# Four-layer graph network, layer 0: padding the rows of four DRAM tables and one SBUF tile, and making a table's second copy on the chip

## The chip, the core and the metric

The kernel runs on one core of one Trainium2 chip. A core has five engines: PE (matrix multiply), DVE and ACT (vector and scalar work), POOL (general elementwise work) and SP, which here only issues transfers. Sixteen DMA engines carry out all transfers, whichever engine issued them. The metric is device time in microseconds (us), from launch to end, and lower is better.

## What is computed

There are 64 graphs (B) of 256 nodes (N) with 256 features (D). Four layers follow one another, and after each comes `x = layernorm(x + layer(x))`. Layer 0 is the one that is changed. It is a recurrence over the nodes; `norm_adjT` is the adjacency transposed and scaled by `dinv`:

```
def step(h, i):
    x = jnp.take(h_e, i, axis=1)
    row = jnp.take(norm_adjT, i, axis=1)
    x_par = jnp.einsum('bj,bjd->bd', row, h)
    iou = x @ W_ioux.T + b_ioux + x_par @ W_iouh.T + b_iouh
    r, z = jnp.split(iou, 2, axis=1)
    r, z = (jax.nn.sigmoid(r), jax.nn.sigmoid(z))
    hc = jnp.tanh(x @ W_coux.T + b_coux + x_par * r @ W_couh.T + b_couh)
    h_new = z * x_par + (1.0 - z) * hc
    h = jax.lax.dynamic_update_slice(h, h_new[:, None, :], (0, i, 0))
```

Step i needs the states that the steps before it have made, so the 256 steps run one after another. Layers 1 to 3 (a graph convolution and two attentions) work on one graph at a time, and have no such order.

## The kernel before

**Setup.** The sums that each node receives from nodes that don't depend on the recurrence are matrix products (`x_product`). They are written to the DRAM table `Us` (`x_out`), for the first half of the nodes before the loop and for the second half inside it (`x_side`).

**The loop.** `for now in range(N)` runs the 256 steps under a schedule written out by hand: what stands first in the text is issued first on its engine. Eight steps (U) make a block, 32 steps (T) a table. Within a step, p is the place in the block and i the place in the table. A step goes from PE to ACT to PE to DVE and back: transpose the parent sum, multiply (`h_part`), sigmoid, transpose, multiply, tanh, combine. On POOL, `ready` (the parent sum of the next step) stands in the same order as POOL's other work.

**Parent sums.** A block's sums stand in a tile `ACC`, loaded from `Us` two blocks ahead (`sums_in`, line L316). Newly made states add to it in three ways:
- near nodes at once, by DVE (`push`, L628) and POOL (`push_far`, L661 and L665);
- states of the last 64 nodes or so by small products on PE (`late`, L519), from the ring of states `Hw` and the masked adjacency table `An`. The result `lb` goes to the DRAM table `Lb` (L499) and comes back as `late_sb` in another layout (L505); POOL adds it in the two last steps of the block before (L874);
- older states by `early_fill` (L418). Their rows `Hs` come from the DRAM table of states `Hd` (`early_load`, issued through `next_load`, L269), the results go to `Es` (L430) and come back as `early_sb` (L447).

**Tables.** For the next table, `late_load` brings the adjacency columns into `raw`, 64 rows in a ring. `raw` is needed twice, in partitions 0 to 63 and 64 to 127, one for each half of the features, so each piece was loaded twice from DRAM, in runs of 32 values. In the steps i = 20 to 22 POOL multiplies `raw` by a mask into `An` (`cut`, L477). `load_S` loads another table once and doubles it by a transfer within SBUF (`S<-S`, L547).

**Transfers.** Nearly all are issued by SP in the order of the text; one that waits holds back those behind it. Transfers for later are put into a list (`load_later`) from which `next_load` takes two in each of the first four steps of a block. New states go into the ring `Hw` by two small transfers a step (`into_ring`, L654), and a quarter of the way from a table's end 32 rows of the ring are written out to `Hd` (`flush`, L636). `load_x` brings the x rows of a block into `xq` (L567).

The DRAM tables `Us`, `Es`, `Lb` and `Hd` are dense. A load that takes eight consecutive rows of 128 values from one of the first three finds 4096 contiguous bytes, and a load of eight rows of 256 values from `Hd` finds 8192; `xq` takes four rows of 1024 bytes into 4096 contiguous bytes of a partition.

**Layers 1 to 3** read `Hd` once more, a graph at a time (`y<-Hd`, L1043).

Of the kernel before, what the change touches and what calls it, by code (L numbers as in the profile page):

```python
# [9 lines left out]
F32 = mybir.dt.float32  # L10
# [9 lines left out]
P = 128  # L20
# [50 lines left out]
def _recurrence(tc, ident, Hd, x, adj, W_ioux, b_ioux, W_iouh, b_iouh, W_coux, b_coux, W_couh, b_couh, wide, then):  # L71
# [19 lines left out]
    nc = tc.nc  # L91
# [12 lines left out]
    with ExitStack() as ctx:  # L104
# [100 lines left out]
        )  # L205

        dram = ctx.enter_context(tc.tile_pool(name="r_dram", bufs=2, space=bass.MemoryType.DRAM))
        Us = dram.tile([2, B, N, P], F32, name="Us", bufs=1)

        def x_product(pb, at, A, Xs):  # L210

# [38 lines left out]
        def next_load(n):  # L250
            if loads:
                loads.pop(0)[1](n)
# [125 lines left out]
        def early_load(e, got=[]):  # L378

            _, k, lo, hi, t = early.pop(e)  # L380
            rows = hi - lo
            if t == 0:
                Es[k, lo] = dram.tile([2, NG, 4, T, P], F32, name=f"Es_{k}_{lo}", bufs=1)
            Hs = wide.tile([P, GB, D], F32, tag="wide", name=f"Hs_{k}_{lo}_{t}")
            last = [load_later(
                Hs[0:rows], Hd[lo:hi, t * GB:(t + 1) * GB, :], 1
            )]
            if t % 2 == 0:
                A = stream.tile([P, 2 * GB, T], F32, tag="A", name=f"A_{k}_{lo}_{t}")
                last.append(load_later(  # L390
                    A[0:rows],
                    adj[t * GB:(t + 2) * GB, lo:hi, k * T:(k + 1) * T].rearrange("b j i -> j b i"), 1
                ))
                got[:] = [A]
            early_in.append((last, k, lo, hi, t, Hs, *got))
# [58 lines left out]
        def late_load(k, n=None):  # L454
# [6 lines left out]
                nc.gpsimd.memset(raw, 0.0)  # L461
            begun = []
            for lo, hi, at in ring(max(first, 0), last):
                for o in range(2):
                    to = raw[o * W + at:o * W + at + hi - lo]
                    of = adj[:, lo:hi, k * T:(k + 1) * T].rearrange("b j i -> j b i")
                    if n is None:
                        nc.scalar.dma_start(to, of)
                    else:
                        begun.append(load_later(to, of, 1.5))  # L470

            def cut(lo):
                while not all(begun):
                    next_load(now)
                part = raw[:, lo:lo + B // 4].rearrange("p b (s u) -> p b s u", u=U)
                take = window[k % 2].rearrange("p (s u) -> p s u", u=U).unsqueeze(1)
                nc.gpsimd.tensor_mul(  # L477
                    An[:, lo:lo + B // 4].rearrange("p b u s -> p b s u"), part,
                    take.to_broadcast(list(part.shape)),
                )  # L480

            for e in range(4):
                if n is None:
                    cut(e * B // 4)
                else:
                    at_step(n + (20, 21, 21, 22)[e], lambda e=e: cut(e * B // 4))
            return An

        def late(first):
# [1 line left out]
            k, i = divmod(first, T)  # L491
            An = tables[k]["An"]
            lb = stream.tile([P, NG, D], F32, tag="lb", name=f"lb_{first}", bufs=1)
            Lb = dram.tile([2, NG, 4, U, P], F32, tag="Lb", name=f"Lb_{first}")
            sides[first] = blk.tile([P, U, P], F32, tag="late", name=f"late_sb_{first}", bufs=1)

            def send():
# [63 lines left out]

        def load_x(a):

            xq = stream.tile([P, U // 2, D], F32, tag="xq", name=f"xq_{a}")
            for h in range(2):
                at = a * U + h * U // 2
                nc.sync.dma_start(xq[h * B:(h + 1) * B], x[:, at:at + U // 2, :])  # L567
            return xq

        def flip_x(a, e, xq):  # L570
# [850 lines left out]
def kernel(ctx: ExitStack, tc: tile.TileContext, ins, out):  # L1421
# [4 lines left out]
    dram = ctx.enter_context(tc.tile_pool(name="dram", bufs=1, space=bass.MemoryType.DRAM))  # L1426
    ident = main.tile([P, P], F32, name="ident")
    make_identity(nc, ident)
    Hd = dram.tile([N, B, D], F32, name="Hd")
    l2, l3 = (  # L1430
        {w + n: ins[f"{l}_gnn_{w}{n}"] for w in "Wb" for n in "vkqo"} for l in ("L2", "L3")
    )
# [55 lines left out]
```

## Time and profile before

| | |
|---|---|
| median of 3 runs | 3435.97 us (3435.91 to 3440.31) |
| the profiled execution | 3432.33 us, its span 3430.6 us |
| granted PE clock in it, mean | 0.968 |
| setup, 0 to 142 us | 142 us, DMA engines 0.97 busy |
| recurrence, 142 to 1560 us | 1418 us, PE 1257.3 us busy, DMA engines 0.66 busy |
| layers 1 to 3, from 1560 us | 1870.6 us, PE 1832.3 us busy, DMA engines 0.20 busy |

The span runs from the first instruction to the last of one execution; the device time has 1.7 us around it. A wait is idle time of an engine ahead of an instruction, with what ended it; `issue` stands for a wait that no event in the profile explains. Queue q1 is that of SP and carries most of the data; q8 and q14 carry instructions. In the transfer view, "under 512 B" and the like count packets cumulatively, and the share is that of the sixteen engines' time in the window.

### The profile page before, as it was taken

How to read it: one execution, taken by the hardware profiler on the slowest of the kernel's cores; microseconds unless marked ns; L12 is line 12 of the kernel's file. 1: busy time of each engine (PE TensorE's matmuls, PEld its weight loads, DVE VectorE, ACT ScalarE, POOL GpSimd, SP SyncE). 2: the span in 40 equal slices, each digit the busy share in tenths (PEclk: the TensorE clock that was granted, in tenths of full speed). 3: DMA queues.
4: the chain of work that ended last, by engine and by line, in shares of the span. 5: the costliest groups of instructions: out<-in, count | busy, mean ns of one | idle time of the engine just before them, and what ended most of it. 6: DMA issues, size and time to landing. Idle time of an engine off the chain costs nothing.

```text
span 3430.6 us, 86707 instructions
## 1 busy us (share of the span) xinstructions
PE 3171.4 (92%) x32424; PEld 2391.6 (70%) x32424; DVE 2571.3 (75%) x7381; ACT 1836.5 (54%) x4754; POOL 1862.5 (54%) x2165
## 2 busy tenths in 40 slices
PE   5699989888888898886999999999999999999997
PEld 4566656555555666665888888888888888888885
DVE  3477767776675777774888888888888888888885
ACT  0154545444444454443666666666666666666664
POOL 2376767766575778762444444444444444444443
PEclk8899999999998999998999999999999999999999
DMA  9856676777987575422122222222222222222210
GB/s 299 227 160 146 167 175 162 166 177 181 205 195 175 143 179 139 128 73 75 47 56 56 56 56 57 58 59 59 58 56 58 56 58 59 56 57 59 57 32 20
DMA packets 595503, 368.82 MB, mean 108 GB/s; under 512 B 282236, under 2 KB 561928, under 8 KB 590344
## 3 DMA queue, kind: packets, MB, share of 16 engines
q1 hardware_dynamic: 576360, 346.19, 40.1%
q10 hardware_dynamic: 18720, 17.04, 1.5%
q8 instruction: 259, 4.24, 0.5%
q14 instruction: 164, 1.34, 0.1%
HBM read 244.45 MB, written 99.61 MB: 100 GB/s over the span
## 4 chain that ended last, share of the span: by engine, by line
PE 79%; DVE 6%; DMA 6%; issue 4%; SPq 2%; POOL 2%; ACT 1%; DVEq 0%; ACTq 0%; POOLq 0%
PE mm L995 13%; PE rc L603 7%; PE rc L595 5%; PE late L519 4%; PE s L1193 4%; PE mm_2f L995 4%; PE mm_3v L995 3%; PE mm_3f L995 3%; PE mm_2v L995 3%; PE mm_t L995 3%; PE mm_2s L995 3%; PE mm_g L995 3%; PE mm_2w L995 3%; PE o L1228 3%; PE z_ps L603 3%
## 5 line engine op out<-in xcount | busy, mean ns | idle before, releaser
L1205 POOL TENSOR_TENSOR p3s<-p 128x256 f32<-128x256 f32 x512 | 358.3, 731 | 365.1 <-ACT p L1203 365.1
L628 DVE SCALAR_TENSOR_TENSOR ACC<-keep,S,ACC 128x128 f32<-128x128 f32 x1712 | 478.8, 342 | 17.3 <-POOL ACC L874 11.7
L995 PE MATMUL mm<-xT,weights 128*128 128x256 f32 x2048 | 484.3, 385 | 2.7 <-ACT xT L1092 2.7
L995 PEld LDWEIGHTS mm<-xT,weights 128*128 128x128 f32 x2048 | 386.7, 191 | 79.9 <-issue 25.5
L1202 DVE TENSOR_TENSOR p<-s,neg 128x512 f32<-128x512 f32 x512 | 317.5, 682 | 118.8 <-PE s L1193 118.8
L665 POOL TENSOR_TENSOR ACC<-ACC,far 128x384 f32<-128x384 f32 (+1 forms) x313 | 371.8, 1188 | 24.5
L803 POOL TENSOR_TENSOR ready<-ACC,dinv 128x128 f32<-128x128 f32 x255 | 101.8, 399 | 378.2 <-DVE ACC L628 370.1
L661 POOL TENSOR_TENSOR far<-hs,S 128x384 f32<-128x384 f32 (+1 forms) x313 | 304.3, 972 | 4.7
L1203 ACT ACTIVATE p<-p 128x512 f32<-128x512 f32 x512 | 292.3, 626 | 1.6 <-DVE p L1202 1.6
L959 ACT ACTIVATE y<-y,shift,rstd 128x256 f32<-128x256 f32 x512 | 272.9, 599 | 26.2 <-DVE shift L957 22.5
L595 PE MATMUL rc<-WxT,xqT 128*64 128x256 f32 x2048 | 283.2, 399 | 1.1 <-issue 1.0
L1117 ACT ACTIVATE qk<-mm,weights 128x256 f32<-128x256 f32 x256 | 107.3, 470 | 301.7 <-PE mm L995 301.7
L1106 POOL TENSOR_TENSOR y<-y,g 128x512 f32<-128x512 f32 x64 | 81.0, 1266 | 301.2 <-issue 301.2
L603 PE MATMUL rc<-WhT,rT 128*64 128x128 f32 x2048 | 176.8, 295 | 54.0 <-DVE rT L826 47.2
L1242 DVE RECIPROCAL rT<-o 128x256 f32<-128x256 f32 x128 | 223.7, 1748 | 0.3 <-PE o L1219 0.2
L822 ACT ACTIVATE rs<-rc 128x128 f32<-128x128 f32 x256 | 70.9, 277 | 283.0 <-PE rc L603 283.0
L519 PE MATMUL late<-Hw,An 64*32 64x128 f32 x7680 | 182.0, 282 | 41.8 <-issue 39.8
L947 DVE BATCH_NORM_STATS2 st<-y 128x6 f32<-128x256 f32 x512 | 209.4, 409 | 13.1 <-POOL y L1106 10.2
L826 DVE TENSOR_TENSOR rT<-rT_ps,xpT 128x128 f32<-128x128 f32 x256 | 74.0, 289 | 181.5 <-PE rT_ps L824 179.8
L951 POOL TENSOR_TENSOR rstd<-rstd,mhalf 128x2 f32<-128x2 f32 x256 | 173.6, 695 | 48.9 <-DVE rstd L950 33.9
L603 PEld LDWEIGHTS rc<-WhT,rT 128*64 128x64 f32 x2048 | 111.7, 141 | 125.0 <-DVE rT L826 93.0
L603 PE MATMUL rc<-WhT,xpT 128*64 128x128 f32 x2048 | 174.6, 291 | 25.8 <-ACT xpT L612 19.1
(162 smaller groups left out, 7347.0 us busy)
## 6 DMA issues: line engine op xcount, KB each, us to landing
xX<-in_x_dram ACTq DMA_DIRECT2D x16, 1024.0 KB, 7.4
Us<-xu SPq DMA_DIRECT2D x64, 256.0 KB, 4.2
xq<-in_x_dram SPq DMA_DIRECT2D x64, 256.0 KB, 6.7
ACC<-Us SPq DMA_DIRECT2D x32, 512.0 KB, 6.5
Es<-eu SPq DMA_DIRECT2D x64, 256.0 KB, 3.3
early_sb<-Es SPq DMA_DIRECT2D x32, 512.0 KB, 5.6
xin<-in_x_dram SPq DMA_DIRECT2D x64, 256.0 KB, 2.9
ad<-in_adj_dram SPq DMA_DIRECT2D x64, 256.0 KB, 3.3
```

Of the source, the lines that this page charges most:

```text
L519: nc.tensor.matmul(pb[o][q * T:(q + 1) * T, e, :], An[rows, b].rearrange("p u s -> p (u s)"), Hw[rows, b, :], start=True, stop=True,)
L595: nc.tensor.matmul(G[o * B:(o + 1) * B], xqT[a, i // 2][:, i % 2, kc, h * B:(h + 1) * B], WxT[:, kc, o, gates], start=False, stop=False, s ...
L603: nc.tensor.matmul(G[o * B:(o + 1) * B], hT[:, kc * B:(kc + 1) * B], WhT[:, kc, o, g], start=False, stop=(kc == 1), skip_group_check=True,)
L628: nc.vector.scalar_tensor_tensor(acc[:, 0, :], keep[:, j % 2, :], s, acc[:, 0, :], ALU.mult, ALU.add)
L661: nc.gpsimd.tensor_mul(tmp[:, 0:count, :], hs.unsqueeze(1).to_broadcast(shape), s.unsqueeze(2).to_broadcast(shape),)
L665: nc.gpsimd.tensor_add(acc, acc, tmp[:, 0:count, :])
L959: nc.scalar.activation(y[:, c, :], y[:, c, :], AF.Identity, bias=shift[:, c:c + 1], scale=rstd[:, c:c + 1],)
L995: nc.tensor.matmul(pm[:, c, :], lhsT[:, k, c * P:(c + 1) * P], rhs[:, k, :], start=(k == 0), stop=(k == 1),)
L1202: nc.vector.tensor_add(p, s_ps[i], self.neg3)
L1203: nc.scalar.activation(p, p, AF.Exp, scale=ISQ)
L1205: nc.gpsimd.tensor_add(both, p[:, 0, :], p[:, 1, :])
L1242: nc.vector.reciprocal(rT, o_ps[:, 1, :])
```

## The change

The four DRAM tables get 64 unused values behind each row, so that a row no longer touches the next, and only the used part is addressed. The tile `xq` gets 4 unused values behind each row. A transfer of several rows, which went in runs of 4096 or 8192 bytes, goes in runs of 512 bytes (`Us`, `Es`, `Lb`) or 1024 bytes (`Hd`, `xq`); the bytes are the same. The adjacency columns are loaded into `raw` once, and a transfer within SBUF copies partitions 0 to 63 to partitions 64 to 127, at step i = 17 of the table before, or for the first table at once.

```diff
-        Us = dram.tile([2, B, N, P], F32, name="Us", bufs=1)
+        Us = dram.tile([2, B, N, P + 64], F32, name="Us", bufs=1)[..., 0:P]
...
-                Es[k, lo] = dram.tile([2, NG, 4, T, P], F32, name=f"Es_{k}_{lo}", bufs=1)
+                Es[k, lo] = dram.tile(
+                [2, NG, 4, T, P + 64], F32, name=f"Es_{k}_{lo}", bufs=1
+            )[..., 0:P]
...
             for lo, hi, at in ring(max(first, 0), last):
-                for o in range(2):
-                    to = raw[o * W + at:o * W + at + hi - lo]
-                    of = adj[:, lo:hi, k * T:(k + 1) * T].rearrange("b j i -> j b i")
-                    if n is None:
-                        nc.scalar.dma_start(to, of)
-                    else:
-                        begun.append(load_later(to, of, 1.5))
-
-            def cut(lo):
+                to = raw[at:at + hi - lo]
+                of = adj[:, lo:hi, k * T:(k + 1) * T].rearrange("b j i -> j b i")
+                if n is None:
+                    nc.scalar.dma_start(to, of)
+                else:
+                    begun.append(load_later(to, of, 1.5))
+
+            def double():
                 while not all(begun):
                     next_load(now)
+                nc.sync.dma_start(raw[W:], raw[0:W])
+
+            def cut(lo):
...
+            if n is None:
+                double()
+            else:
+                at_step(n + 17, double)
...
-            Lb = dram.tile([2, NG, 4, U, P], F32, tag="Lb", name=f"Lb_{first}")
+            Lb = dram.tile([2, NG, 4, U, P + 64], F32, tag="Lb", name=f"Lb_{first}")[..., 0:P]
...
-            xq = stream.tile([P, U // 2, D], F32, tag="xq", name=f"xq_{a}")
+            xq = stream.tile([P, U // 2, D + 4], F32, tag="xq", name=f"xq_{a}")
...
-                nc.sync.dma_start(xq[h * B:(h + 1) * B], x[:, at:at + U // 2, :])
+                nc.sync.dma_start(xq[h * B:(h + 1) * B, :, 0:D], x[:, at:at + U // 2, :])
...
-    Hd = dram.tile([N, B, D], F32, name="Hd")
+    Hd = dram.tile([N, B, D + 64], F32, name="Hd")[:, :, 0:D]
```

## The prediction

> **What bounds the kernel now.** I read the stage table first, then PE's waits in the long middle stage, then the transfers in windows with and without those waits, then SP's rows.
>
> ```profile
> q8 instruction: 259, 4.24, 0.5%
> ...
> 0.00:142.00 142.00, 81.71 (x319) 64.30 (x320) 39.66 (x62) 4.54 (x7) 29.39 (x23) 0.81 0.97 291
> 142.00:1560.00 1418.00, 1257.34 (x19819) 852.13 (x19817) 1034.72 (x3608) 658.07 (x2186) 981.20 (x1055) 0.96 0.66 159
> 1560.00:3430.60 1870.60, 1832.30 (x12290) 1475.18 (x12290) 1496.87 (x3711) 1173.86 (x2561) 851.88 (x1088) 0.99 0.20 55
> ```
>
> Columns: window, PE, weight loads, DVE, ACT, POOL (busy, instructions), granted clock, DMA share, GB/s. Layers 1 to 3 are PE at work (1832 of 1871 us) with idle DMA engines: nothing is to be had there. The recurrence has 161 us in which PE is idle. Queue q8 carries 4.24 MB in 259 packets. PE has 32,424 matmuls and as many weight loads, 65 bytes each on that account: q8 is PE's instruction fetch, 250 instructions a packet.
>
> ```profile
> PE late L519 <- issue: 39.8, 22, 6.4
> PE rc L603 <- issue: 10.8, 7, 3.0
> PE z_ps L603 <- issue: 9.3, 4, 3.7
> PE z_ps L595 <- issue: 8.1, 3, 4.8
> PE rc L595 <- issue: 1.0, 1, 1.0
> ...
> 508.31 0.65 PE L519 MATMUL late<-Hw,An 64*32 64x128 f32 x8 [6.36 <-issue]
> ```
>
> These 37 waits (69.0 us) have no releaser. The last line shows one: it falls inside 32 equal products on tiles long at hand, so no operand can be missing. What can be missing is the instruction. Two windows in which the DMA engines are full tell when:
>
> ```profile
> DMA packets 1049, 1.56 MB, mean 156 GB/s; under 512 B 831, under 2 KB 831, under 8 KB 911
> q1 hardware_dynamic: 1047, 1.54, 104.0%
> q8 instruction: 1, 0.02, 1.1%
> ...
> DMA packets 3214, 2.16 MB, mean 308 GB/s; under 512 B 44, under 2 KB 3069, under 8 KB 3213
> q1 hardware_dynamic: 3213, 2.14, 100.4%
> q8 instruction: 1, 0.02, 0.9%
> ```
>
> The first is 496 to 506 us, before the 6.36 us wait: 80 packets of 2 to 8 KB and 138 of 8 KB or more (one is the fetch) carry nearly all the bytes. The second is 813 to 820 us, a flush of `Hd` in runs of 512 bytes: just as full, twice the rate, and PE has no wait at all. Over more places:
>
> ```profile
> sum 90.00, PE 57.07 PEld 38.07 DVE 51.05 ACT 28.00 POOL 42.01; mean PE 6.34 PEld 4.23 DVE 5.67 ACT 3.11 POOL 4.67
> ...
> sum 49.00, PE 48.57 PEld 34.15 DVE 33.12 ACT 25.19 POOL 33.88; mean PE 6.94 PEld 4.88 DVE 4.73 ACT 3.60 POOL 4.84
> ```
>
> The first sums nine 10 us windows with long runs in flight (from 314 us to 1248 us; DMA share 0.88 to 1.08, 126 to 236 GB/s): PE idle 33 of 90 us. The second sums the seven flush windows (share 0.78 to 1.02, 202 to 314 GB/s): idle 0.4 of 49 us. The bound that can move is therefore PE's fetch behind full queues, worst behind long runs.
>
> **The change part by part.**
>
> *Long runs split.* Engine time per byte: the flush window spends 1.004 x 16 x 7 = 112 us on 2140 kB, 53 ns per kB; the first window 166 us on 1540 kB, 108 ns per kB; 909 to 917 us (161 packets of 8 KB or more and 139 of 4 KB, 102.3%, 1.88 MB) 70. The fetch itself took 1.1% of 160 us, 1.8 us, in the first and 0.9% of 112, 1.0 us, in the flush. Split are all 64 loads of `Hs` (36.9 MB), 94 of `ACC`, `early_sb`, `late_sb` (49 MB) and 64 of `xq`; the runs of `rows` (4096), `S` and `raw` (128) and the copies within SBUF stay. What can be won: 69.0 us of waits, and the slow clock after them (508.3 to 513.3 us has 0.67), for which I put 0.7 us on each of the 22 or so over 1.2 us: 15. Ceiling 84. By bytes, some 90% of the first window is split, less elsewhere, and raw, S and rows still fill the queue: I take 60%, -50 us. Bounds: 0 (delay set by bytes queued, whatever the run) and -84, or -104 with some 20 us of waits on `Lb`, `Hs` and `Hw` transfers standing in those queues.
>
> Two rules of the Trainium skill speak against this. "Runtime: NRT & Kernel Launch", Instruction fetch mechanics, says that refills of 256 instructions are prefetched and their cost mostly hidden: by it the term is 0 and the whole change +8. The refill size agrees (250); the hiding does not (69 us), and the row decides. "DMA: Bandwidth & Descriptors", Why small descriptors are slow, charges each packet about 3 cycles over its bytes/32: 19 for 512 bytes, 131 for 4096, so 16% more per byte; on 49 MB at about 310 GB/s (159 us of all engines) that is an estimated +22 us of DMA time. A lone 128-partition load of 4096-byte runs reaches 350 to 440 GB/s in its best slices (206 to 212 us), against 300 to 350 for the flush: that agrees, 0.3 us a load, +29 us for 94. But the mixed windows above, where it matters, pay 70 to 108 ns per kB: 36.9 MB of `Hs` at 17 ns less (70 to 53) is 627/16 = -39 us. Net about 0, and with 34% of DMA time idle none of it is on the path, except `late_sb`: 30 loads 0.3 us later, of which the waits show three ending a POOL wait: +1.
>
> *Raw loaded once.*
>
> ```profile
> L269 SPq DMA_DIRECT2D raw<-in_adj_dram x26: 343/2564/11215, 148.7 to 1279.9; - x26
> L636 SPq DMA_DIRECT2D Hd<-Hw x24: 609/1196/7390, 266.8 to 1534.0; - x24
> L316 SPq DMA_DIRECT2D ACC<-Us x32: 377/414/1879, 130.0 to 1440.3; - x32
> S<-S SPq DMA_DIRECT2D x7, 328.0 KB, 8.9
> ```
>
> SP is held 2.6 us (median) by each of 26 loads; 13 go, 8 copies come: SP issues 5 transfers fewer, ACT one fewer. Some 28,700 packets of 128 bytes go, 512 of 8192 bytes come. SP's hold was not on the path: 0 for it; what the queue gains is in the 60%. The copy (512 KB) has no row; the nearest is `S<-S`, 3.9 us in quiet (256 KB), 8.9 in traffic (328 KB). By bytes 8 to 14 us. It is issued at i = 17 and POOL wants it at i = 20, three steps of 4.9 us: cover 14.7. Ready copies cost 0; if one lands late, POOL waits at `cut`, behind it stands `ready`, and DVE and PE wait for that. Six tables by 0 to 3 us: 0 to +18, I take +3. Behind the copy on SP stand `rows`, `A`, `Hs`, `xq` of that step, wanted a block later: 0.
>
> *First table.* Here the wait is on the path:
>
> ```profile
> 129.89 11.80 DMA raw<-in_adj_dram
> ...
> 141.82 4.99 POOL An L477 x4
> ...
> 146.87 1.80 POOL raw L461
> 148.67 0.37 POOL ready L803
> ```
>
> One load instead of two should land between 135.5 (half) and 141.7; then SP's copy of 512 KB, 5 to 9 us: ready 1 us earlier to 9 later; I take +4. SP waits meanwhile with the side loads `xA`, `xX`, `rows` behind it, first used at 159 us: 0.
>
> *No cost:* the stores to the padded tables go in the same 512-byte runs; PE reads the same rows of `xq`; `y<-Hd` keeps 1024-byte runs, with PE's 1832 us as cover (2.8 us to landing, a graph ahead; exposed, 64 x some tenths).
>
> Sum against the profiled execution: 3432.3 - 50 + 1 + 3 + 4 = 3390. The median of the runs stands 3.6 us above that execution: 3394.
>
> **The rivals.**
> 1. *The fetch is delayed by the bytes ahead of it, not by the run.* For it: a fetch also waits when 128-byte runs fill the queue, and a packet of several short runs may hold an engine as long as one long run did. Against: the flush windows. Then only the halved `raw` helps, at most 28,700 x 16 ns/16 = 29 us of DMA time, perhaps 8 us of waits, against +8: 3436.
> 2. *Slower: packets hold SP.* The transfers of many packets (`raw` up to 3072, `Hd` up to 2048) hold SP up to 11.2 and 7.4 us; `ACC` with 128 only 0.4. After the change `ACC`, `early_sb` and `late_sb` have 1024 and `Hs` up to 896. A block issues five or six of them just ahead of `Lb` and `Hw`. If each holds SP 1 to 2 us more, `Lb` goes some 6 us later and `late_sb` misses POOL's addition. The slack there is about 7 us in a good block (issued 1165.3, 5.0 to landing, added 1177.0) and none in the worst. At 3 us over, in 30 blocks, +90: 3394 + 90 - 40 (queue thinner) = 3444. It decides once holds exceed the slack by 1.5 us on average. Against: SP's holds are mostly the same bytes draining, and these drain faster.
> 3. *Raw copies land late in every table*: 15 us after issue plus 8 would cancel the gain; `raw` itself took 14.3 at most. 3436 to 3445.
> 4. *Nearly all fetch waits go*, and the transfer waits with them: 3345.
>
> **How the numbers follow.** Forecast (and the part of 4 on its side) 0.75; rival 1 0.10, of which half within the band; rival 2 0.11; rival 3 0.04. About 0.2%, 7 us, is what can be told from no change. Faster by more: 0.75 and a little of rival 1, 0.77; the same 0.06; slower 0.17. The range reaches from rival 4 a little beyond (the -104 bound gives 3340) to the first third of the slower cases: 3335 to 3444.
>
> **What would show it.** PE's waits on issue in the recurrence fall from 69 to under 30 us; q1 has about 677,000 packets instead of 576,360 (84,000 more for 94 loads, 32,000 for `Hs`, 12,000 for `xq`, 28,000 fewer for `raw`) at nearly the same bytes; bursts at i = 1 to 3 and 9 to 11 move over 250 GB/s; layers 1 to 3 keep 1871 us. I am wrong in the size if the waits on issue stay above 50 us (rival 1), in the sign if POOL's waits on `late_sb` (11.8 us now) grow past 60 (rival 2) or its waits on `raw` past 50 (rival 3).

## The result: no change, where 42 us less were forecast

The changed kernel took 3438.93 us (median of its runs, 3417.72 to 3454.21) beside 3435.92 us of the kernel before on the same chip. The ratio is 1.001, with a 95% interval of 0.9988 to 1.0032: no change that can be told. The forecast was 3394. The profiled execution below is the slowest of the changed kernel's runs (3454.21 us), so up to 15 us of it are its own; times are compared by medians further down.

The changed kernel's first queue and its stages (columns as before: window, then PE, weight loads, DVE, ACT, POOL, granted clock, DMA share, GB/s):

```profile
q1 hardware_dynamic: 677912, 346.85, 41.4%
```

```profile
142.00:1580.00 1438.00, 1258.70 (x19805) 853.89 (x19804) 1031.84 (x3608) 658.30 (x2185) 980.95 (x1055) 0.95 0.69 157
1580.00:3452.40 1872.40, 1834.89 (x12290) 1475.65 (x12290) 1495.55 (x3711) 1175.07 (x2561) 851.79 (x1088) 0.99 0.20 55
```

The change does what it says: 677,912 packets, where the prediction had about 677,000. Layers 1 to 3 keep their length (1872 us; 1871 before). So everything happens in the recurrence, where PE's waits in 142 to 1580 us are now these (engine, tile and line, what it waited for, us in total, times, longest). `rc` on `rT` is the step's own product that waits for the transposed factor which DVE hands it:

```profile
PE rc L611 <- DVE rT L834: 65.7, 62, 7.8
PE late L527 <- issue: 37.6, 18, 5.4
...
PE xpT_ps L618 <- DVE xp L872: 11.4, 24, 5.0
PE z_ps L611 <- issue: 7.9, 3, 3.6
PE early L420 <- DMA Hs<-Hd: 7.9, 3, 6.9
PE early L420 <- DMA A<-in_adj_dram: 5.0, 3, 3.6
PE rc L611 <- issue: 4.7, 5, 1.7
PE z_ps L603 <- issue: 3.7, 1, 3.7
```

With one of 0.6 us that is left out, the waits on issue come to 54.5 us, down from 69.0. The forecast wanted them under 30. And others grew: the early product's waits on transfers were 3.7 us before, and `rc` on `rT` was

```profile
PE rc L603 <- DVE rT L826: 47.2, 59, 6.3
```

Ahead of `rT` stands POOL's addition of the late sums. Its waits, before and after:

```profile
POOL ACC L874 <- DMA late_sb<-Lb: 11.8, 3, 8.0
POOL ACC L874 <- DMA Hw<-hs: 3.6, 1, 3.6
...
POOL ACC L882 <- DMA Hw<-hs: 22.0, 3, 10.7
POOL ACC L882 <- DMA late_sb<-Lb: 19.4, 6, 5.4
```

15.4 us became 41.4. (The addition reads nothing of `Hw`. The profile infers what ended a wait, and both lines are waits of this addition.) A part of the expected gain is there, and other waits have grown beside it. The chain that ended last shows a third thing, at the first table (start, us, what):

```profile
131.18 6.61 DMA raw<-in_adj_dram
137.87 1.41 DMA raw<-raw
139.28 5.39 issue
144.68 4.99 POOL An L481 x4
```

One load is shorter than two (6.61 us against 11.80), but behind it come the copy and 5.39 us to which the profile gives no cause; the trace has no landing time for this copy, so they may be the copy itself still under way. `An` starts at 144.68 us in place of 141.82.

### The profile page after: what moved, and what is told of

Read it like the earlier page. It is cut to its first block, busy times and chain, and to the rows that moved or that the text cites. A ratio compares the mean times of both kernels' runs of the same rounds, so it can differ in the third digit from the quotient of the medians.

```text
span 3452.4 us, 86708 instructions
## 1 busy us (share of the span) xinstructions
PE 3175.9 (92%) x32424; PEld 2394.5 (69%) x32424; DVE 2565.6 (74%) x7381; ACT 1838.4 (53%) x4754; POOL 1862.0 (54%) x2165
## 3 DMA queue, kind: packets, MB, share of 16 engines
q1 hardware_dynamic: 677912, 346.85, 41.4%
## 4 chain that ended last, share of the span: by engine, by line
PE 79%; DVE 7%; DMA 6%; issue 4%; POOL 2%; SPq 1%; ACT 1%; DVEq 0%; POOLq 0%; ACTq 0%
PE mm L1003 13%; PE rc L611 7%; PE rc L603 5%; PE s L1201 4%; PE late L527 4%; PE mm_2f L1003 4%; PE mm_3v L1003 3%; PE mm_t L1003 3%; PE mm_3f L1003 3%; PE mm_2v L1003 3%; PE mm_g L1003 3%; PE mm_2s L1003 3%; PE mm_2w L1003 3%; PE o L1236 3%; DVE ACC L636 3%
## 5 line engine op out<-in xcount | busy, mean ns | idle before, releaser
L636 DVE SCALAR_TENSOR_TENSOR ACC<-keep,S,ACC 128x128 f32<-128x128 f32 x1712 | 479.3, 343 | 38.6 <-POOL ACC L882 32.9
L955 DVE BATCH_NORM_STATS2 st<-y 128x6 f32<-128x256 f32 x512 | 209.6, 409 | 16.5 <-POOL y L1114 13.8
L1072 POOL TENSOR_TENSOR dis<-dis,mhalf 128x2 f32<-128x2 f32 x64 | 44.8, 700 | 275.2 <-DVE dis L1071 263.0
```

The source lines that it names most:

```text
L636: nc.vector.scalar_tensor_tensor(acc[:, 0, :], keep[:, j % 2, :], s, acc[:, 0, :], ALU.mult, ALU.add)
```

## The experiments

All ratios are to the kernel before on the same chip and in the same job, with 95% intervals; "us" is the ratio's distance from 1 times 3433. An interval is 7 to 12 us wide, that of the change 15. Sums of waits come from one profile each, and single executions of one kernel differ by 10 us and more. How far such sums wander shows in two kernels below whose transfers are those of before (`Us` made larger, and 64 small products ahead): their waits on issue are 73.1 and 72.0 us for 69.0, POOL's on `late_sb` and `Hw` 13.2 and 28.8 for 15.4. So only larger shifts are read.

| kernel | ratio | interval | us |
|---|---|---|---|
| the change | 1.0010 | 0.9988 to 1.0032 | +3 |
| Hd, xq padded | 1.0005 | 0.9994 to 1.0017 | +2 |
| Us, Es, Lb padded | 0.9949 | 0.9931 to 0.9967 | -17.5 |
| Us, Es padded | 0.9962 | 0.9948 to 0.9976 | -13 |
| Es, Lb padded | 0.9963 | 0.9949 to 0.9977 | -13 |
| Es padded | 0.9961 | 0.9946 to 0.9976 | -13 |
| Us padded | 1.0029 | 1.0017 to 1.0040 | +10 |
| all five padded, raw as before | 0.9988 | 0.9975 to 1.0001 | -4 |
| raw once, copied | 1.0051 | 1.0034 to 1.0069 | +17.5 |
| raw once, first table twice | 1.0026 | 1.0011 to 1.0040 | +9 |
| the same, copies in 512 bytes | 1.0002 | 0.9992 to 1.0013 | +1 |

### The three parts

One part of the change alone in each. Rows of `Hd` and `xq` padded, for runs of 1024 bytes:

```
-    Hd = dram.tile([N, B, D], F32, name="Hd")
+    Hd = dram.tile([N, B, D + 64], F32, name="Hd")[:, :, 0:D]
...
-            xq = stream.tile([P, U // 2, D], F32, ...)
+            xq = stream.tile([P, U // 2, D + 4], F32, ...)
```

> The kernel before with Hd and xq padded alone (runs of 1024 bytes instead of 8192 and 4096). Theory R: PE's waits on issue in the recurrence fall to 40 us or less and the time by 25 us or more (ratio 0.993). Theory B: waits on issue within 15 us of the 69 us before, time within 8 us. Theory G (fetch gains are given back, because the transfers that PE and POOL wait for land later): waits on issue fall by about 15 us, the waits on late_sb, Hs and Hw together rise by as much, time within 8 us.

Rows of `Us`, `Es` and `Lb` padded, for runs of 512 bytes:

```
-        Us = dram.tile([2, B, N, P], ...)
+        Us = dram.tile([2, B, N, P + 64], ...)[..., 0:P]
...
-                Es[k, lo] = dram.tile([2, NG, 4, T, P], ...)
+                Es[k, lo] = dram.tile([2, NG, 4, T, P + 64], ...)[..., 0:P]
...
-            Lb = dram.tile([2, NG, 4, U, P], ...)
+            Lb = dram.tile([2, NG, 4, U, P + 64], ...)[..., 0:P]
```

> The kernel before with Us, Es and Lb padded alone (runs of 512 bytes instead of 4096). Theory R: waits on issue fall by some 10 us, time by 5 to 15 us. Theory B: no fall. Theory G: SP's hold on ACC and what follows grows (ACC above 0.8 us median), Lb is issued later, POOL's waits on late_sb rise from 11.8 us to 25 or more, and the time rises by 5 to 20 us.

The raw loads once, with the copy in SBUF:

```
-                for o in range(2):
-                    to = raw[o * W + at:o * W + at + hi - lo]
+                to = raw[at:at + hi - lo]
...
+                nc.sync.dma_start(raw[W:], raw[0:W])
```

> The kernel before with raw loaded once and copied within SBUF alone. Theory R and B alike: the first table's copy costs 4 to 8 us at steps 1 and 2; 28,700 packets of 128 bytes fewer relieve the queue and save 0 to 15 us of waits on issue later. Theory G: the copy of 512 KB at i = 17 delays what is queued behind it and nothing is saved: time 0 to 10 us above before. Sum of the parts: if the three parts alone add up to the change within 10 us, no part needs another.

Measured +2, -17.5 and +17.5 us. The sum, +2, is close to what the change as a whole does (+3), but by chance: the last section of runs shows that the parts don't add. A gain of two fifths of the forecast's 42 us was there in one part, the long loads of `Hs` gave none of it, and the raw copies alone cost as much as was gained. The waits of PE on issue in the one profile of each were 61.4, 52.7 and 77.4 us against 69.0.

### What the raw copies cost

The first table loaded twice as before; the later ones loaded once and copied.

```
                 if n is None:
                     nc.scalar.dma_start(to, of)
+                    nc.scalar.dma_start(raw[W + at:W + at + hi - lo], of)
...
-            if n is None:
-                double()
-            else:
-                at_step(n + 17, double)
+            if n is not None:
+                at_step(n + 17, double)
```

> The kernel before, with only the raw copies changed, and those only from the second table on: the first table is loaded twice by ScalarE's queue as before, each later one is loaded once and copied within SBUF in 64 runs of 8192 bytes. The same with the first table copied as well was 17.5 us slower than before, ratio 1.0051. Theory one (the first table's load followed by its copy, in series, delays the first steps: step 8 ended 4.8 us later there, and the steps of the first table took 13.5 us more in all): this run is 4 to 7 us slower than before, and the first eight steps are back at 38.7 us. Theory two (the copy's long packets hold up TensorE's instruction fetch in every table): this run keeps 12 us or more of the 17.5, and the waits of TensorE on issue stay near 77 us, against 69 before. The forecast's own term for these copies, +3 us over all tables and +4 for the first, would give 3 us.

The same with the copy in four transfers of 512-byte runs:

```
-                nc.sync.dma_start(raw[W:], raw[0:W])
+                quarters = raw.rearrange("p (a c q) t -> p c a (q t)", a=4, c=4)
+                for c in range(4):
+                    nc.sync.dma_start(quarters[W:, c], quarters[0:W, c])
```

> As the run beside it (first table loaded twice, later ones loaded once and copied within SBUF), but each copy goes as four transfers of 64 x 4 runs of 512 bytes in place of one transfer of 64 runs of 8192 bytes. Theory two (the 8192-byte packets, some 600 ns each, hold up TensorE's fetch): the waits on issue fall back to 69 us or less, and the time falls by 5 to 10 us against the run beside it. If the copy costs by its bytes, or by when it is made, the two runs agree within 3 us; if three more issues on SP's queue matter, this run is slower by up to 3 us.

The first table, loaded twice again, gives back 17.5 - 9 = 8.5 us (the two intervals together leave this open by some 8 us); the copies in short runs give back the other 8 (by 6). PE's waits on issue in the recurrence, first with the copies in runs of 8192 bytes:

```profile
PE late L524 <- issue: 49.6, 28, 6.5
...
PE z_ps L608 <- issue: 13.8, 6, 4.2
```

and with the copies in runs of 512:

```profile
PE late L526 <- issue: 43.4, 25, 6.7
...
PE rc L610 <- issue: 13.0, 6, 4.9
```

With the waits of the other lines on issue (22.5 us there, 13.8 here) that is 85.9 us against 70.2: with the long copies they are 17 us above the kernel before (8 above it in the run with raw loaded once throughout, which has the same later copies), with the short ones level with it. POOL, whose `cut` uses the copies, waits for no copy in either. So the later copies' price is not that they land late; the waits point to the fetch of instructions, which the long form holds up.

### The fetch measured by itself

Three kernels with nothing on PE but products of the late product's shape, and stages with one form of transfer each on SP's queue; nothing of the reference is computed. In the first, all matmuls read the same 64 rows. The profile shows two instructions for each of these matmuls (and two weight loads), of 53 ns here (191.0 us for 3584), so that 256 instructions last 6.8 us:

```
+            nc.tensor.matmul(pt[q * 32:(q + 1) * 32, e, :], w[0:64, :], h[0:64, :], ...)
```

> A kernel of its own that computes none of the four layers: twelve stages, each of 1792 small products on PE (the form of the late products, 64x32 weights, 128 columns, 14 fetches of 256 instructions) that need no data, beside 14 MB of one kind of transfer kept queued on SP: none; 112 or 128 rows of 8192 bytes and the same in runs of 1024; 128 rows of 4096 and the same in runs of 512; 64 rows of 4096 and of 1024; the raw load (48 rows, 128-byte runs); the flush (512-byte runs); the copy within SBUF. Theory R (the forecast's: long runs delay the fetch): the stage beside 8192-byte runs takes at least 1.5 times as long as that beside 1024-byte runs on the same rows, that beside 4096 at least 1.3 times that beside 512. Theory B (what is queued delays the fetch, whatever the run): each pair within 15%, every loaded stage clearly above the stage with none. Theory H (rows in fewer partitions make packets slow, not their length): 112 rows move fewer GB/s than 128 rows at either run length, and 64 rows fewer still.

The order of transfers across stages was not held, so they ran ahead of the matmuls, and several forms fell into one stage. But in the trace they follow one another: 112 rows in runs of 8192 bytes land until 58.3 us, 112 rows in 1024 until 120.6, 128 rows in 8192 until 151; and from 220 to some 345 us come 128 rows in 1024, 4096 and 512. (Here: window, length, PE and weight loads, then DVE, POOL, clock, DMA share, GB/s.)

```profile
58.30:120.60 62.30, 51.84 (x947) 43.00 (x943) 0.00 (x0) 0.00 (x0) 1.00 1.10 242
120.60:151.00 30.40, 30.40 (x576) 26.71 (x572) 0.00 (x0) 0.00 (x0) 1.00 0.92 384
224.70:415.70 191.00, 190.99 (x3584) 190.93 (x3584) 0.00 (x0) 0.00 (x0) 1.00 0.67 231
```

Beside 128 rows PE doesn't lose a tenth of a microsecond, in runs of 8192 bytes or of 512. Beside 112 rows it waits: 8 times, 10.5 us in all, in the 62 us with runs of 1024 bytes, and 3 times, 3.2 us, in the 48 us before them with runs of 8192. (112 rows move 242 GB/s here, 128 rows 384, as theory H had it.) In this kernel PE takes longer over its instructions than a fetch lasts undisturbed, as in the four layers, where the kernel before has 259 fetches in 3430.6 us, one in 13 us. With that slack it is the rows, and not long runs, that bring the waits.

In the second kernel the order is held, and the matmuls rotate over row halves and column groups, so that PE waits for every fetch; 16 MB of one form in each stage:

```
+    ctx.enter_context(tc.manual_schedule())
...
+                rows = slice(o * 64, (o + 1) * 64)
+                nc.tensor.matmul(pb[o][q * 32:(q + 1) * 32, e, :], w[rows, :], h[rows, :], ...)
```

> A stream of matmuls of the late product's shape, 2048 to a stage and nothing else on TensorE, with 16 MB of one form of transfer on SP's queue in each stage: loads of 112 or 128 rows in runs of 8192 or 1024 bytes, of 128 rows in runs of 4096 or 512, of 64 rows in 4096 or 1024, raw loads in runs of 128, a store in runs of 512, and copies within SBUF in runs of 8192 or 512. Nothing of the kernel is computed. By the forecast (long runs delay the fetch of instructions) a stage beside long runs shows two or more times the issue waits of the same bytes in short runs, for every pair. By its rival (the bytes queued delay it) the stages of a pair agree within a fifth. If only transfers within SBUF or stores to DRAM delay the fetch, the load pairs agree and the copy pairs differ.

The stages in order: no transfer; 112 rows in runs of 8192, then 1024; 128 rows in 8192, then 1024; 128 rows in 4096, then 512; 64 rows in 4096, then 1024; 48 rows in 128; a store in 512; copies within SBUF in 8192, then 512; no transfer. Each has 2048 matmuls, shown as 4096; the second number is its length, the last but one the share of time in which the DMA engines were busy:

```profile
4.60:122.10 117.50, 72.46 (x4096) 63.63 (x4096) 0.02 (x1) 3.05 (x1) 0.93 0.02 4
125.80:280.60 154.80, 82.40 (x4096) 73.12 (x4096) 0.00 (x0) 0.00 (x0) 0.81 0.42 115
284.50:434.80 150.30, 81.88 (x4096) 71.84 (x4096) 0.00 (x0) 0.00 (x0) 0.83 0.46 119
438.70:573.20 134.50, 78.90 (x4096) 69.52 (x4096) 0.02 (x1) 0.00 (x0) 0.85 0.31 128
577.00:715.30 138.30, 78.81 (x4096) 68.61 (x4096) 0.00 (x0) 0.00 (x0) 0.84 0.36 125
719.10:853.30 134.20, 79.84 (x4096) 69.82 (x4096) 0.00 (x0) 0.00 (x0) 0.84 0.32 129
857.20:992.80 135.60, 79.23 (x4096) 69.01 (x4096) 0.00 (x0) 0.00 (x0) 0.87 0.45 127
996.60:1155.50 158.90, 86.51 (x4096) 77.08 (x4096) 0.00 (x0) 0.00 (x0) 0.77 0.53 109
1159.50:1319.50 160.00, 85.39 (x4096) 74.54 (x4096) 0.00 (x0) 0.00 (x0) 0.78 0.61 108
1323.30:1486.90 163.60, 95.56 (x4096) 84.93 (x4096) 0.00 (x0) 0.00 (x0) 0.73 0.89 106
1490.80:1634.50 143.70, 81.44 (x4096) 72.13 (x4096) 0.00 (x0) 0.00 (x0) 0.85 0.49 120
1638.50:1792.70 154.20, 83.31 (x4096) 74.36 (x4096) 0.00 (x0) 0.00 (x0) 0.81 0.53 111
1796.60:1923.50 126.90, 78.92 (x4096) 68.46 (x4096) 0.00 (x0) 0.00 (x0) 0.87 0.55 136
1927.50:2047.50 120.00, 72.58 (x4096) 63.35 (x4096) 0.00 (x0) 0.00 (x0) 0.93 0.02 4
```

Read the pairs. For loads the run length makes little difference to the stage: 154.8 and 150.3, 134.5 and 138.3, 134.2 and 135.6, 158.9 and 160.0 us, now one longer, now the other. What makes one is the number of rows: 16 MB over 128 rows cost 16 to 20 us above the quiet stages (118.75 us, their mean), over 112 rows 32 to 36, over 64 rows 40 to 41. Two things are in that. With fewer rows the same bytes take longer: by the trace they are done after 41 to 56 us, 62 to 65, and 81 to 86. And each fetch takes longer meanwhile. PE gets 256 instructions every 3.7 us in the quiet stages, every 5.0 to 6.2 us beside 128 rows, every 7.3 to 7.8 beside 112 and 7.6 to 7.9 beside 64 (medians). PE in the first of these kernels needed 6.8 us for 256, which fits that 128 rows cost it nothing and 112 rows did.

Only for copies within SBUF do the two forms differ: 154.2 us in 8192 bytes, 126.9 in 512. But they differ in more than the run. The long copies fill the engines for 81 us; the short ones, four transfers each, keep them 0.58 busy for 115. So it is not shown whether long packets or full engines are the reason. The kernel's seven later tables copy 7 x 512 KB, 3.67 MB; by these two stages that is 27.3 x 3.67/16.8 = 6 us, beside the 8 measured there.

A third kernel was to give the fetch slack beside transfers that begin at a mark, by letting half of the matmuls run at 53 ns:

```
+                half = o if m // 16 % 2 else 0
+                rows = slice(half * 64, (half + 1) * 64)
```

> A stream of 4096 matmuls to a stage of the late product's shape, half of them so placed that they take 53 ns and half that take 27, so that 256 instructions last some 5.1 us where an undisturbed fetch comes every 3.5: a stage without transfers takes about 165 us. In each other stage one transfer of 512 KB (896 KB for 112 rows, 384 KB for raw) is begun after every 96 matmuls (192 for 112 rows) by VectorE's mark. Nothing of the kernel is computed. With PE always waiting for its fetch, loads of the same bytes in long and short runs had cost the same (134.0 and 135.4 us for 128 rows in runs of 4096 and 512). If the stall is what a fetch's lag has over the slack, and long runs make few long lags and short runs many short ones, the stage of 4096-byte runs is longer than that of 512 by 3 us or more here. If lag goes with bytes alone, they agree within 2 us, and what the 512-byte reads gain in the kernel (0.19 us each) comes from elsewhere. The copies within SBUF should differ by far more: some 20 us or more for runs of 8192 against 512.

The pair of loads agrees again (128 rows in 4096 bytes 255.4 us, in 512 bytes 254.5) and that of copies differs (262.9 and 251.3). But the stage without transfers took 236.9 us. The expectation's 165 us missed that 4096 matmuls are 8192 instructions; at 53 and 27 ns by halves they would have lasted 330. 236.9 us are 3.7 us for 256 instructions, as in the stream without slack: PE still waited for its fetches, so this kernel says nothing on slack, and the first of the three remains the one that does.

### Which of the padded reads gain

Seven runs on the 17.5 us. `Us` and `Es` padded as above, `Lb` as before:

> The kernel before with the rows of Us and Es padded (reads of 4096-byte runs become runs of 512 bytes), Lb left as it was. With Lb padded too it was 17.5 us faster than before, ratio 0.9949. Lb is a third of the three buffers' reads per step or less, and it is the one with a deadline a step away. If the gain comes from the fetch of instructions beside 4096-byte runs, it goes with the bytes and this run keeps 11 to 14 us of it; if it comes from the late pair's own trip through DRAM (late_sb landing sooner), this run is within 4 us of before.

Only the line of `Us` changed:

> The kernel before with the rows of Us alone padded: 32 of the 94 reads of 512 KB that went in runs of 4096 bytes and now go in runs of 512. Us and Es together gained 13.2 us, with Lb 17.5. If the gain is per read (0.19 us each, fetch or other), this run is 5 to 8 us faster than before. If it is made at one place (early_sb or late_sb landing with its deadline near), Us is the one of the three whose data is wanted latest, and this run is within 3 us of before.

Only the line of `Es`, and the lines of `Es` and `Lb`:

> The kernel before with the rows of Es alone padded. Us and Es together were 13.2 us faster than before, Us alone 9.7 us slower. If the parts add, each with a cost of its own: 23 us faster, ratio 0.9933. If each is a shift of bursts against the fetch of instructions whose size is not the part's own, anything between 20 us faster and 10 slower, and the middle (8 us faster, by bytes a half of the pair) is as likely.

> The kernel before with the rows of Es and Lb padded, Us left as it was. If the parts add (-17.5 for the three, less +9.7 for Us): 27 us faster, ratio 0.992, the fastest so far. If they don't, about the 17.5 us of the three together or less.

The four with `Es` padded and `Hd`, `xq` and raw as before lie together (-13, -13, -13, -17.5 us, with intervals that overlap), and `Us` alone is slower by 10, so the padded `Es` is the gain, and here too the parts don't add: 23 and 27 us were expected of the last two by addition. `Us` made larger without padding its rows tells whether addresses do it:

```
-        Us = dram.tile([2, B, N, P], F32, name="Us", bufs=1)
+        Us = dram.tile([3, B, N, P], F32, name="Us", bufs=1)[0:2]
```

> The kernel before with Us made half as large again by a third block that is never used (16.8 MB become 25.2, as in the padded form), its rows left contiguous: reads stay in runs of 4096 bytes, and only the addresses of the buffers behind it move. If run length is the cause of what Us did when padded (+9.7 us), this run equals before within 2 us; if the addresses are, it is slower by 5 to 10.

Ratio 0.9998 (0.9983 to 1.0014): where the later buffers lie does nothing. And `early_sb` in runs of 512 bytes with `Es` as it was:

```
-                    part = blk.tile([P, U, P], F32, tag="early", ...)
+                    part = blk.tile([P, U, P + 2], F32, tag="early", ...)[:, :, 0:P]
```

> The kernel before with the rows of the tile that receives the early sums padded in SBUF by 8 bytes (128 + 2 numbers to a row) and Es in DRAM left contiguous: early_sb's 32 reads go in runs of 512 bytes from unchanged addresses. Es padded in DRAM alone was 13.4 us faster. If the run length makes that gain, this run is 10 to 16 us faster than before; if the stride of the rows in DRAM does, it equals before within 3 us.

Ratio 0.9992 (0.9976 to 1.0008), 3 us: the shorter runs alone are not what gains 13. It has the same 605,032 packets on q1 as the kernel with `Es` padded in DRAM. What is left is the row stride in DRAM (24 KB for 16), or the rows of 520 bytes in SBUF taking something back; this stays open. The profiles don't help: POOL's waits on `late_sb` are 2.3 us with `Es` padded in DRAM and 21.4 in SBUF, but 1.2 and 21.6 in the two kernels whose transfers are those of before.

Whether such differences come merely from where the fetches fall among the steps was tried by 64 small products ahead of everything:

```
+        for _ in range(64):
+            nc.tensor.matmul(pw, ident, ident[:, 0:8], start=True, stop=True)
```

> The kernel before with 64 matmuls (and 64 weight loads) of 8 columns put before the first product, on a bank that nothing reads, in a time when TensorE waits for its first transfer; every fetch of 256 instructions then falls 128 instructions elsewhere in the steps, and no transfer changes. By their own work 0 to 3 us more. If where fetches fall against the bursts moves the time by as much as the parts of the change did, it differs from before by 5 us or more, either way; if the kernel is steady against that, it is within 3 us.

Ratio 1.0028 (1.0016 to 1.0039), 10 us slower. It was not the clean shift that it was meant to be: the first step's `rs` came at 152.5 us in its profile and at 142.7 in that of before, so in that execution the setup alone lost as much as the medians differ. It leaves open how sensitive the recurrence is.

### Where the rest went: the parts together

The change with the two costs of its raw copies mended, by the edits of the run with short copies:

```
-                nc.sync.dma_start(raw[W:], raw[0:W])
+                for c in range(4):
+                    nc.sync.dma_start(quarters[W:, c], quarters[0:W, c])
...
+                    nc.scalar.dma_start(raw[W + at:W + at + hi - lo], of)
```

> The changed kernel with two things taken back or altered: the first table is loaded twice as before, and each later copy goes as four transfers of 512-byte runs in place of one of 8192-byte runs. Everything else of the change stays (Us, Es, Lb, Hd and xq padded). If the raw copies are all that ate the gain of the change: 15 us faster than before (-17.5, +1.7 for Hd and xq, +0.8), ratio 0.9955, against the changed kernel's 1.001. If Hd and xq in runs of 1024 cost more beside the other padded buffers than alone (more packets held on SP's queue): between 10 us faster and no change.

That without the lines of `Hd` and `xq`, so 512-byte reads and mended copies:

```
-    Hd = dram.tile([N, B, D + 64], F32, name="Hd")[:, :, 0:D]
+    Hd = dram.tile([N, B, D], F32, name="Hd")
...
```

> The kernel before with Us, Es and Lb padded (reads of 512-byte runs), the first table loaded twice as before, and each later table loaded once and copied in four transfers of 512-byte runs. Apart, the two parts were 17.5 us faster and 0.8 us slower than before. If they add: 16 to 17 us faster, ratio 0.995. If both draw on the same waits of TensorE's fetch, more reads in short runs make room for the copies and the sum is better than 17.5; if the fuller queue of SP gives the gain back, it is under 10 us faster.

And the change with raw as before:

```
-                to = raw[at:at + hi - lo]
+                for o in range(2):
+                    to = raw[o * W + at:o * W + at + hi - lo]
...
-                nc.sync.dma_start(raw[W:], raw[0:W])
```

> The changed kernel with its raw loads put back as before (each table loaded twice, the first by ScalarE's queue), so that only the padded rows (Us, Es, Lb, Hd, xq) are left. If the parts add: 3.4 - 17.5 = 14 us faster than before, ratio 0.996. With the copies in 512-byte runs in place of the second loads it had been 6 us faster (0.9982). If Hd and xq in 1024-byte runs take back the gain of the 512-byte reads when both are there, it is 0 to 6 us faster.

The first is 6 us faster than before (0.9982, 0.9969 to 0.9996) where 15 were expected by addition, the second 10 (0.9971, 0.9955 to 0.9987) for 17, the third 4 (0.9988, 0.9975 to 1.0001) for 14 to 16. The third is the purest case, padding and nothing else. PE's waits in its recurrence:

```profile
PE rc L605 <- DVE rT L828: 73.0, 69, 5.5
...
PE late L521 <- issue: 13.3, 14, 4.7
PE xpT_ps L612 <- DVE xp L866: 12.2, 32, 4.3
PE late L521 <- DMA Hw<-hs: 10.9, 7, 3.9
...
PE early L420 <- DMA Hs<-Hd: 6.6, 1, 6.6
PE rc L605 <- issue: 5.0, 4, 2.4
PE z_ps L597 <- issue: 5.0, 3, 2.9
PE rc L597 <- issue: 4.8, 3, 4.3
PE z_ps L605 <- issue: 4.6, 3, 2.2
```

The waits on issue are 33.0 us (with one of 0.3), not 69.0, 36 us less; the two halves of the padding alone had 7.6 and 16.3 less. But `rc` on `rT` rose from 47.2 to 73.0, `late` on `Hw` from 1.5 to 10.9, `xpT_ps` on `xp` from 7.9 to 12.2, `early` on `Hs` from 3.7 to 6.6, and `rc` on `ACC` from 2.4 to 4.2: +44. POOL's addition waits, and DVE waits for the addition, here and before:

```profile
POOL ACC L876 <- DMA late_sb<-Lb: 29.0, 9, 7.1
POOL ACC L876 <- DMA Hw<-hs: 21.2, 4, 7.2
...
DVE ACC L630 <- POOL ACC L876: 39.9, 12, 6.5
...
DVE ACC L628 <- POOL ACC L874: 11.7, 4, 6.2
```

What stands ahead of them is SP. By the trace, the time from the last copy into `lb` to SP's issue of `late_sb`, summed over the 30 blocks, is 180 us before; 192 with `Hd` and `xq` padded, 194 with `Us`, `Es`, `Lb`; and 221, 229 and 245 us in the three kernels with all five padded (the change, its mended form, and this one). In every other kernel it is under 200. POOL's two waits go with it: 15.4; 19.1 and 24.2; 41.4, 42.8 and 50.2, in every other kernel under 30. DVE's waits for the addition too: 11.7; 16.1 and 18.6; 32.9, 35.0 and 39.9, in every other kernel under 23. In the worst block SP sends `Lb` 13.4 us after `lb` is ready, 7.3 before, because it is still busy with a flush of `Hd`, loads of `dinv`, and `Hs`, `A` and `xq`.

SP is later because its issues hold it longer. Summed over its issues in 142 to 1575 us of each trace, the raw loads left out (they stand at other steps), it is held 854 us before, 928 with `Hd` and `xq` padded, 906 with `Us`, `Es`, `Lb`, and 974 with all five: these holds add, and POOL's waits don't. The change and its mended form have 969 and 987 us, their copies within SBUF counted. Up to some 74 us more of holds cost POOL little; 115 and more cost it 26 to 35 us. That is how the parts come to more together than apart. No run lengthened the holds and nothing else, so this is read from traces that agree, not tested by itself.

Whose packets lengthen a hold is another matter. SP's rows for `ACC` (duration least, median, most in ns), in this kernel, with `Us` alone padded, and with `Es` alone padded:

```profile
L316 SPq DMA_DIRECT2D ACC<-Us x32: 502/1294/5396, 131.7 to 1446.8; - x32
...
L316 SPq DMA_DIRECT2D ACC<-Us x32: 379/420/4911, 130.8 to 1446.6; - x32
...
L316 SPq DMA_DIRECT2D ACC<-Us x32: 455/897/3563, 129.9 to 1427.2; - x32
L507 SPq DMA_DIRECT2D late_sb<-Lb x30: 581/586/1115, 207.8 to 1508.7; - x30
```

With `Us` padded `ACC` itself goes in 1024 packets and is issued as quickly as before (420 ns, 414 before). With `Es` padded `ACC` still has 128, and takes 897. 24 of its 32 issues follow directly on `early_sb`, and it is `early_sb` that then has 1024. So the hold of a transfer of many packets is paid, here, by the issue behind it. (The last row, of the kernel with all five, is `late_sb`'s own: 586 ns for 426.)

## Why the prediction was wrong, point by point

The step that failed is the sum for the padded rows, -50 for the fetch and +1 for `late_sb`. With raw loaded as before, the padding measured -4 us (-9 to 0). The raw part did about what was forecast: +7 in the sum, and the change lies 8 us (by 9) above the kernel with the padding alone, each taken against the kernel before.

- *`late_sb`, +1.* This is the term that turned the result. The prediction let the extra packets cost nothing, since a third of the DMA time is idle, "except `late_sb`: 30 loads 0.3 us later". It counted how much longer a load takes, and not how much later SP issues it. The issues come later by 42 us in the change and by 66 in the padded kernel, summed over the blocks, and POOL's waits on them rose by 26 and 35 us, PE's waits other than on issue by 44 in the latter. Rival 2 had the mechanism and the place (packets hold SP, `Lb` goes late, POOL misses its data). It was wrong in whose issue pays for `ACC` (its hold follows `early_sb`'s packets), and it had put the point at which it decides at waits on `late_sb` above 60 us. With those on `Hw` they are 41 in the change and 50 in the padded kernel, and that is enough to cancel the gain. The prediction treated forecast and rival as alternatives; both came.
- *Waits on issue, -50 us.* They did fall: by 36 us in the padded kernel's profile, by 14.5 in that of the change. The raw copies put some back. With the copies in short runs the profile of the whole change still has 49.3 us, and only raw loaded as before has 33.0, so it is not the long form alone. The prediction had counted the raw part as a relief for the queue.
- *"Worst behind long runs".* The reading of the windows failed here. The windows with long runs were loads of `Hs`, of at most 112 rows; the flush windows, with no wait, were stores in short runs. Rows and direction changed along with the run length. Measured by themselves, 112 rows delay a fetch beyond the 6.8 us that PE needs for 256 such instructions, in long and short runs (7.8 and 7.3 us). 128 rows don't (5.0 to 6.2), nor does the store in runs of 512 (5.1). Splitting `Hs` alone (with `xq`) left the time where it was.
- *The cost of splitting, net 0.* In the isolated stages of 128 rows the engines were busy for 0.45 and 0.32 of the time with the same bytes in runs of 512 and 4096, 0.36 and 0.31 in 1024 and 8192. Less the 0.02 of a quiet stage, and times the stage's length, short runs take 45% more engine time (0.43 x 135.6 against 0.30 x 134.2) and 21% more. The estimate from the Trainium skill ("DMA: Bandwidth & Descriptors", Why small descriptors are slow), 3 cycles for each packet, was 16% for the first, too little here. The prediction's own 24% less for `Hs` has no counterpart in any run: for 112 rows it is 0.44 x 150.3 against 0.40 x 154.8, 7% more.
- *Raw copies, +3; first table, +4.* With nothing else changed they cost some 8 us each, more than forecast. Rival 3's late landings were not the reason: POOL waited for a copy once, 7.7 us, at the first table of the run with raw alone changed. There the load and the copy stand in series, as foreseen (`An` starts 2.9 us later in the change). At the later tables the long form of the copy is the reason.
- *Layers 1 to 3, 0*, and the packet count: as predicted.

Shown: that the padding as a whole gains about nothing, the price of the copies' form, that rows and not the run length of loads bring the fetch's delay in two isolated streams, and that `late_sb` is issued later and waited for longer in the three kernels with all five padded and in no other. Argued only: that SP's holds are the whole cause of that; and that long packets, and not full engines, are what is dear in the copies. Open: why the waits on issue fell by 36 us in the padded kernel, when run length does so little in the isolated streams (PE may have waited for `rT` meanwhile, while the fetch went on); and why `Es` padded in DRAM gains 13 us and `Us` alone loses 10.

The best version is then the smallest: pad `Es` alone (0.9961), or with `Us` and `Lb` (0.9949); their intervals overlap. Both beat the kernel before and the change.

## What to carry to other kernels

When two kinds of windows differ in a wait, list everything in which they differ (rows, direction, run length) before naming the cause; a stream that changes one of them at a time costs a single run. For a queue that issues for everyone, measure how late it sends the piece with the deadline, from the moment its data is ready; a change that lengthens each issue can cost little until the sum passes some point, so try the parts of such a change one by one and keep those that pay. And parts that are measured alone can add up to the right sum by chance: the run with all but one of them tells.

## What was not expected of the hardware

- With nothing in the queues, the isolated stream of late products still ran at the pace of its fetch: 4096 matmul instructions and as many weight loads in 117.5 us, PE busy in 72.5 of them, the rest waits on issue. At 256 instructions a packet (447 packets for 114,688 instructions in the whole run) that is one in 3.7 us.
- A fetch takes longer the fewer rows the loads beside it have: 256 instructions every 5.0 to 6.2 us beside loads of 128 rows, 7.3 to 7.9 beside 112 or 64 rows, whatever the run length.
- A copy of 16 MB within SBUF delays the isolated stream by 35 us in runs of 8192 bytes and by 8 in runs of 512, in four transfers for one.
- An issue can be held by the transfer ahead of it: `ACC`'s took 420 ns at the median when its own packets had grown eightfold, and 897 when those of `early_sb` had.
